# Graph network with cross-attention on one core: turned rows moved into the values' products, weight sums moved to the pair's sums, scores held behind the weighted values, last bias moved into the feed-forward

## The chip, the core and the metric

The kernel runs on 1 core of one Trainium2 chip. Its time is the device time of one execution in microseconds (us); for a set of runs the median is given. Five engines matter: PE (TensorE: matmuls and transposes; PEld is its weight load), DVE (VectorE), ACT (ScalarE), POOL (GpSimd) and SP (SyncE, which here issues nearly all DMAs). Each executes its own instructions in a fixed order and waits on semaphores for the others.

## The reference

N = 1024 rows of D = 512 features pass a layer norm with ReLU, a batch norm and a graph convolution. Then come L = 4 layers, each a cross-attention (16 groups of 64 rows, each with its own M = 256 condition rows, H = 8 heads of DH = 64) and a gated feed-forward block. A second graph convolution and two residuals end it.

```python
for i in range(L):
    a = _attn(_ln(h, ln2_w[i], ln2_b[i]), cond, Wq[i], Wk[i], Wv[i], Wo[i])
    h = h + a
    u = _ln(h, ln3_w[i], ln3_b[i]) @ geglu_w[i] + geglu_b[i]
    val, gate = jnp.split(u, 2, axis=-1)
    f = val * jax.nn.gelu(gate, approximate=False)
    h = h + f @ ffo_w[i] + ffo_b[i]
```

All of it is float32. The bias `ffo_b[i]` is added to `h` once in each layer; nothing reads `h` between the attention's end and the feed-forward's sums except the layer norm of `ln3`, which must not see the bias.

## The kernel before

**Tiling.** The 1024 rows are 8 blocks of 128 rows, `h[0]` to `h[7]`, views of one tile `hall`. A block is also an attention step g (0 to 7): two groups of 64 rows. Most matrix products are done in seven block products instead of eight (Strassen's scheme in Winograd's form), so sums of blocks are made beside them: of weights and of turned rows mostly on POOL, of products on DVE (read from PSUM, where matmuls write), with copies on ACT.

**One attention step** `g` of layer `l` (the loop from line 1198 on): `scores` (L750) multiplies queries by keys of step g (tiles `sc`, L761) and does the softmax: on DVE the row maximum (L768), on ACT the exponential (L773), on DVE the reciprocal (L776) and the scaling of the probabilities (L778, eight instructions of 128x256 from SBUF to SBUF). `kv` (L745) then makes the keys and values of step g+1 with two calls of `seven` (L708): products 0, 5, 6, 4, 1, 3, 2 go to the PSUM banks `pa`, `pb`, `pc`, `pd`, `pa`, `pc`, `pd`, eight matmul records each. In between, DVE makes `u2` (L721) and `u3` (L724) and adds them into the four quarters of the result. Product 3 is accumulated onto `pc`, so it can begin only when `u3` has read that bank. Last, `mix` (L782) turns the probabilities of step g (tiles `tr_pr`, copied out as `pT`, L809 on DVE and L811 on ACT) and weighs the values with them (tiles `po`, L795); its result is `oT`.

**Between the keys and the values** of step g+1 stands `between` (L1207). At every second step `attn_out_pair` (L836) multiplies the two last `oT` with `wo`, again in seven products (`wab`, `wcd`): four sums on POOL ahead of them (L843 to L846, "the pair's sums"), and on POOL again the additions L865, L866, L871 and L874, which finish `h` of two blocks. Then `ln3_norm` (L1175) normalises one finished block (two at step 6) on DVE, from the statistics (L151) to the scaled rows `xn` (L172), and `ln3_bias` (L1184) adds `ffb`, the feed-forward's output bias, to `h` of that block on POOL (L1185). `ln3_turn` (L1187) turns the normalised rows on PE (`tr_ln`, four transposes a block, L184) and writes them to `ln3T` with two ACT and two DVE instructions (L698, L696); `ln3_sums` (L1191) makes the sums `ln3S` of blocks 4 and 5 on POOL (L212 to L215, eight instructions).

**Steps 6 and 7.** At step 6 the first feed-forward weights, `wval` and `wgate`, are loaded and `geglu_weights` (L887) makes their sums `ges` on POOL (L219 to L222, 128x1024 each). In the program that call stands behind `kv`. Step 7 stands behind the loop: its scores, `attn_out` of block 6 (`pw`, L824), the first feed-forward products (`Quad.first`, tiles `ga`) as a filler, `mix`, then the last two blocks.

**The feed-forward** has R = 4 rounds r: four `Quad`s each (tiles `ga` to `gd`), then `ffn_out` twice (tiles `fa` to `fd`), which adds to `h` on DVE and POOL. POOL also makes the weight sums of the rounds to come.

**What sets the order.** The framework places each engine's instructions in one order when the kernel is built, by a simulated execution: of the instructions that the simulation holds ready, the one that is earliest in the program comes first. `tc.issue_after` forbids one engine's instruction to come ahead of another. Tiles of a pool (36 `slots`, 8 PSUM banks) are given out in the order in which the program first writes them, so an instruction that first writes a tile is never placed ahead of an earlier first write of that pool. On the chip the order is fixed, and an instruction waits only for what it really needs, so an engine can run well ahead of the simulation. `ges`, the keys `kT`, the values `v`, `ln3T`, `ln3S` and all weights are tiles of `slots`.

## Time and profile before

| | us |
|---|---|
| median of 3 runs | 2541.16 (2541.14 to 2543.61) |
| the profiled execution, whole | 2541.56 |
| its span, first to last instruction | 2539.7 |
| DVE busy | 1405.7 (55%) |
| POOL busy | 643.4 (25%) |
| ACT busy | 556.2 (22%) |

The profiled execution lies 0.40 us above the median of the runs. A row of a timeline has the start in us from the span's start, the time in us, the engine, the source line, the operation, the tiles (out <- in), the shapes and a count; in brackets stands how long the engine sat idle before it, and for whom. A row of the list of waits has who waited for whom, the total in us, how often, and the longest. Rows that stand together with a count are records: a float32 matmul leaves two. The four layers are alike; in time, layers 2 and 3 repeat layer 1 with a shift of about 588 us each.

### The profile page before, as it was taken

Reading aid. Unit: us, or ns where it says so; the run is one execution under the profiler, and the core shown is the slowest. Engines: PE = TensorE matmul, PEld = TensorE weight load, DVE = VectorE, ACT = ScalarE, POOL = GpSimd, SP = SyncE. Lnnn points to the kernel's source line nnn. Section 1 sums busy time; section 2 is a strip of 40 time slices with the busy share of each in tenths; the row PEclk is TensorE's granted clock in tenths of the full one; section 3 lists DMA queues with packets and bytes.
Section 4 is the critical chain, followed back from the end, with each engine's and each line's share of the span. In section 5 each row is a group of like instructions: output and inputs, shape, how many; then the busy total and the mean of one; then the engine's idle time right before and its main releaser. Section 6 shows DMA issues by size and latency. Waiting matters only on the chain. (4 is left out here: it accounts for less than half of the span.)

```text
span 2539.7 us, 32198 instructions
## 1 busy us (share of the span) xinstructions
PE 2512.0 (99%) x12464; PEld 1770.6 (70%) x12464; DVE 1405.7 (55%) x3030; ACT 556.2 (22%) x1318; POOL 643.4 (25%) x535
## 2 busy tenths in 40 slices
PE   8999999999999999999999999999999999999999
PEld 5778886666578887655587888556676888566565
DVE  9655566544574556544474556644484455654561
ACT  7322222111122222111122222111112222211111
POOL 0322225422210113433320113333320111531410
PEclk9999999999999999999999999999999999999999
DMA  6312231111121111210212111110112121111020
GB/s 178 130 38 84 92 133 63 34 50 37 59 66 68 51 54 51 71 33 17 95 38 79 59 63 51 54 50 17 59 67 75 42 80 60 41 34 62 13 87 34
DMA packets 67136, 156.81 MB, mean 62 GB/s; under 512 B 5576, under 2 KB 5904, under 8 KB 66976
## 3 DMA queue, kind: packets, MB, share of 16 engines
q1 hardware_dynamic: 64880, 149.25, 17.9%
q0 software_dynamic: 1376, 4.30, 0.5%
q8 instruction: 103, 1.69, 0.3%
q10 hardware_dynamic: 720, 1.11, 0.1%
q14 instruction: 57, 0.47, 0.1%
HBM read 133.66 MB, written 20.97 MB: 61 GB/s over the span
## 5 line engine op out<-in xcount | busy, mean ns | idle before, releaser
L301 PE MATMUL ga<-ln3T,wval 128*128 128x512 f32 x512 | 233.9, 593 | 0.0
L923 ACT ACTIVATE g<-g,gcols 128x512 f32<-128x512 f32 x128 | 92.4, 722 | 431.8 <-DVE g L936 367.2
L301 PEld LDWEIGHTS ga<-ln3T,wval 128*128 128x128 f32 x512 | 96.0, 190 | 109.9 <-issue 109.0
L773 ACT ACTIVATE pr<-sc,nmax 128x256 f32<-128x256 f32 x256 | 118.2, 474 | 180.0 <-DVE nmax L768 180.0
L997 POOL TENSOR_TENSOR hall<-fu,hall 128x512 f32<-128x512 f32 x24 | 30.5, 1270 | 468.0 <-DVE fu L996 468.0
L301 PE MATMUL pa_v<-wv,ct 128*128 128x256 f32 x512 | 123.1, 379 | 0.0
L301 PE MATMUL fa<-wff,fT 128*128 128x256 f32 x512 | 121.6, 379 | 0.0
L301 PE MATMUL gc<-ln3S,wgate 128*128 128x512 f32 x256 | 120.4, 592 | 1.1 <-DVE gu L933 1.1
L301 PE MATMUL pd_k<-ct,wks 128*128 128x256 f32 x512 | 121.0, 379 | 0.0
L301 PE MATMUL pd_v<-wvs,ct 128*128 128x256 f32 x512 | 121.0, 379 | 0.0
L301 PE MATMUL pc_k<-ct,wk 128*128 128x256 f32 x512 | 120.9, 379 | 0.0
L301 PE MATMUL pc_v<-wv,ct 128*128 128x256 f32 x512 | 120.9, 379 | 0.0
L301 PE MATMUL gb<-ln3S,ges 128*128 128x512 f32 x256 | 120.6, 593 | 0.0
L301 PE MATMUL gd<-ln3T,ges 128*128 128x512 f32 x256 | 120.5, 593 | 0.0
L301 PE MATMUL gd<-ln3S,ges 128*128 128x512 f32 x256 | 120.3, 592 | 0.0
L301 PE MATMUL gc<-ln3T,wgate 128*128 128x512 f32 x256 | 120.3, 592 | 0.0
L301 PE MATMUL pa_k<-ct,wk 128*128 128x256 f32 x480 | 116.2, 385 | 0.0
L301 PEld LDWEIGHTS fa<-wff,fT 128*128 128x128 f32 x512 | 97.3, 190 | 21.8 <-issue 9.6
L1185 POOL TENSOR_TENSOR hall<-hall,ffb 128x512 f32<-128x512 f32 x28 | 36.1, 1294 | 286.9 <-DVE xn_ln L172 286.9
L301 PEld LDWEIGHTS pd_v<-wvs,ct 128*128 128x128 f32 x512 | 97.3, 190 | 13.2
L301 PEld LDWEIGHTS pc_k<-ct,wk 128*128 128x128 f32 x512 | 97.3, 190 | 13.2
L301 PEld LDWEIGHTS pd_k<-ct,wks 128*128 128x128 f32 x512 | 97.3, 190 | 13.2
(319 smaller groups left out, 4866.7 us busy)
## 6 DMA issues: line engine op xcount, KB each, us to landing
ct<-cond_dram SPq DMA_DIRECT2D x72, 512.0 KB, 4.7
wval<-in_L_gnn_geglu_w_dram SPq DMA_DIRECT2D x32, 512.0 KB, 4.7
wgate<-in_L_gnn_geglu_w_dram SPq DMA_DIRECT2D x32, 512.0 KB, 4.7
wff<-in_L_gnn_ffo_w_dram SPq DMA_DIRECT2D x32, 512.0 KB, 4.5
cond_dram<-ct SPq DMA_DIRECT2D x24, 512.0 KB, 3.6
cond<-in_L_gnn_cond_dram SPq DMA_DIRECT2D x32, 256.0 KB, 4.5
ct<-cond_dram SPq DMA_DIRECT2D x24, 256.0 KB, 4.9
wk<-in_L_gnn_Wk_dram SPq DMA_DIRECT2D x8, 512.0 KB, 5.2
```

Source lines behind the costliest of these rows:

```text
L301: nc.tensor.matmul(at, left[:, k, l0:l1], right[:, k, r0:r1], start=start and n == 0 and k == 0, stop=n == len(cols_of) - 1 and k == 1, sk ...
L773: nc.scalar.activation(pr3[:, a, :], ps3[:, a, :], AF.Exp, bias=nmax[:, a:a + 1], accum_out=tot[:, a:a + 1])
L923: nc.scalar.activation(pre, pre, AF.Gelu, bias=gcols[:, cg:cg + 1])
L997: t.tensor_tensor(h21, halves_of(u2), h21, OP.add)
L1185: t.tensor_tensor(h[nb], h[nb], ffb, OP.add)
```

## The change

Four edits, all of order; each arithmetic operation is done as before, on the same shapes, but the bias of all eight blocks is now added on POOL.

1. `seven` gets a hook `late`, called behind product 1; with the values of step g+1 it turns the rows that `between` has normalised. Before, they were turned behind the values.
2. `attn_out_pair` is split: `pair_sums` has the four POOL sums. At step 6 `geglu_weights` is called between `pair_sums` and the pair's products.
3. The score matmuls of step g (from 1 on) may not be placed ahead of the last matmul of `mix` of step g-1.
4. `ln3_bias` is gone, on POOL behind each normalised block and on DVE for block 7. The eight additions stand on POOL in round 1 of the feed-forward.

```diff
@@ seven
+        late()
         product(3, c, False)
@@ scores
+                        with tc.issue_after(mix.last.ins) if g else nullcontext():
                             nc.tensor.matmul(
@@ mix
-                            nc.tensor.matmul(
+                            mix.last = nc.tensor.matmul(
@@
-    def attn_out_pair(l, g, oTs, right):
+    def pair_sums(l, g, oTs):
...
         t.tensor_tensor(s2, s1, a11, OP.subtract)
         t.tensor_tensor(s4, a12, s2, OP.subtract)
-        left = [a11, a12, s4, a22, s1, s2, a21]
+        return [a11, a12, s4, a22, s1, s2, a21], more[:, M:]
+
+    def attn_out_pair(l, g, left, p1, right):
@@ ln3_norm
-            for nb in blocks:
-                ln3_bias(nb)
-
-        def ln3_bias(nb, t=nc.gpsimd):
-            t.tensor_tensor(h[nb], h[nb], ffb, OP.add)
@@ between
                 if len(oTs) == 2:
-                    attn_out_pair(l, g - 2, oTs, wo7)
+                    blocks = pair_sums(l, g - 2, oTs)
                     oTs.clear()
+                    if g == NG - 2:
+                        left = geglu_weights(l, 0, *raw)
+                    attn_out_pair(l, g - 2, *blocks, wo7)
                 ln3_norm(*ready, behind=last_key)
 
             if g or l:
-                kv_next = kv(l, g + 1, wk, wv, between)
+                kv_next = kv(l, g + 1, wk, wv, between, late=lambda: [ln3_turn(nb) for nb in ready])
             else:
                 kv_next = kT_1, values(0, 1, wv)
-            if g == NG - 2:
-                left = geglu_weights(l, 0, *raw)
             save_conds()
             next_cond(l, g + 2)
             for nb in ready:
-                ln3_turn(nb)
                 if nb >= 4:
                     ln3_sums(nc.gpsimd, nb)
@@ block 7
-        ln3_bias(g, nc.vector)
@@ rounds of the feed-forward, behind the weight sums of the round
+            if r == 1:
+                for nb in range(NB):
+                    nc.gpsimd.tensor_tensor(h[nb], h[nb], ffb, OP.add)
```

More of the change, by code (lines that the diff above doesn't have):

```diff
@@ L284, in next_cond @@
             conds[l, g] = load_cond(l, g) if l else prepare_cond(g)
-    conds = {}
+    conds, left = {}, None
     def blocks_of_w(w):
@@ L706, in weight_sums, with seven @@
         return [blk[0], blk[1], s4, blk[3], s1, s2, blk[2]]
-    def seven(name, product, c11, c12, c21, c22, s1=None, beside=lambda ins: None):
+    def seven(name, product, c11, c12, c21, c22, s1=None, beside=lambda ins: None,
+              late=lambda: None):
         b, c, d = (bank(f"{n}_{name}") for n in ("pb", "pc", "pd"))
@@ L737, in keys, with values, kv @@
         return kT, seven(f"k_{l}_{g}", of_k(wk, conds[l, g]), *blocks_out(kT), s1, *beside)
-    def values(l, g, wv, begun=None):
+    def values(l, g, wv, begun=None, **also):
         v, s1 = begun or (slots_of(2, f"v_{l}_{g}"), None)
         v11, v21, v12, v22 = blocks_out(v)
-        seven(f"v_{l}_{g}", of_v(wv, conds.pop((l, g))), v11, v12, v21, v22, s1)
+        seven(f"v_{l}_{g}", of_v(wv, conds.pop((l, g))), v11, v12, v21, v22, s1, **also)
         return v
-    def kv(l, g, wk, wv, between):
+    def kv(l, g, wk, wv, between, **also):
         kT, last_key = keys(l, g, wk)
         between(last_key)
-        return kT, values(l, g, wv)
+        return kT, values(l, g, wv, **also)
     def scores(l, g, qT, kT):
@@ L760, in scores @@
                     for b in range(2):
-                        nc.tensor.matmul(
-                            banks[2 * c2 + j][b * NPG:(b + 1) * NPG, a * M:(a + 1) * M],
-                            qT[g // 4][c2][pj, a, c0 + b * NPG:c0 + (b + 1) * NPG],
-                            kT[c2][pj, a, b * M:(b + 1) * M], start=True, stop=True)
+                        with tc.issue_after(mix.last.ins) if g else nullcontext():
+                            nc.tensor.matmul(
+                                banks[2 * c2 + j][b * NPG:(b + 1) * NPG, a * M:(a + 1) * M],
+                                qT[g // 4][c2][pj, a, c0 + b * NPG:c0 + (b + 1) * NPG],
+                                kT[c2][pj, a, b * M:(b + 1) * M], start=True, stop=True)
         for u in range(4):
@@ L794, in weigh @@
                             at = (a * MB + m) * P + b * NPG
-                            nc.tensor.matmul(
+                            mix.last = nc.tensor.matmul(
                                 po[j * DH:(j + 1) * DH, n0:n0 + NPG],
@@ L846, in attn_out_pair @@
         t.tensor_tensor(s4, a12, s2, OP.subtract)
-        left = [a11, a12, s4, a22, s1, s2, a21]
+        return [a11, a12, s4, a22, s1, s2, a21], more[:, M:]
+    def attn_out_pair(l, g, left, p1, right):
+        n = f"{l}_{g}"
+        t = nc.gpsimd
         ab, cd = bank(f"wab_{n}"), bank(f"wcd_{n}")
@@ L855, in attn_out_pair @@
         kept = acc_tile(f"ou_{n}")
-        p1, u2, p7 = more[:, M:], kept[:, :M], kept[:, M:]
+        u2, p7 = kept[:, :M], kept[:, M:]
         product(0, a, True)
@@ L1207, in between @@
             def between(last_key):
+                nonlocal left
                 if len(oTs) == 2:
-                    attn_out_pair(l, g - 2, oTs, wo7)
+                    blocks = pair_sums(l, g - 2, oTs)
                     oTs.clear()
+                    if g == NG - 2:
+                        left = geglu_weights(l, 0, *raw)
+                    attn_out_pair(l, g - 2, *blocks, wo7)
                 ln3_norm(*ready, behind=last_key)
             if g or l:
-                kv_next = kv(l, g + 1, wk, wv, between)
+                kv_next = kv(l, g + 1, wk, wv, between, late=lambda: [ln3_turn(nb) for nb in ready])
             else:
                 kv_next = kT_1, values(0, 1, wv)
-            if g == NG - 2:
-                left = geglu_weights(l, 0, *raw)
             save_conds()
```

## The prediction, made before the changed kernel was run

> **What bounds the kernel now.** I read the page's first part, then the list of PE's waits, then PE's timeline in layer 1.

> ```profile
> PE 2512.0 (99%) x12464; PEld 1770.6 (70%) x12464; DVE 1405.7 (55%) x3030; ACT 556.2 (22%) x1318; POOL 643.4 (25%) x535
> PE po L795 <- DVE pT L809: 3.0, 4, 0.8
> ```

> PE is the bound: outside 27.7 of 2539.7 us it has a matmul in work. None of the four edits takes work off PE, so all they can win are waits and badly placed instructions, and all they can lose is a new wait of PE. The second row is the one wait of the layers that comes every time: 0.75 us in each, before `po`. More is hidden inside the busy time, and only the timeline shows it: first three rows of an ordinary step, then step 6, then step 7's `mix`.

> ```profile
> 950.86 2.08 PE L795 MATMUL po<-pT,v 128*64 128x64 f32 x64
> 952.88 1.96 PE L761 MATMUL sc<-kT,qT 64*64 64x256 f32 x32
> 954.77 1.99 PE L301 MATMUL pa_k<-ct,wk 128*128 128x256 f32 x8
> ...
> 963.50 1.89 PE L301 MATMUL pc_k<-ct,wk 128*128 128x256 f32 x8
> ...
> 981.63 1.89 PE L301 MATMUL pc_v<-wv,ct 128*128 128x256 f32 x8
> ...
> 985.09 1.04 PE L184 MATMUL tr_ln<-ident,xn_ln 128*128 128x128 f32 x8
> ...
> 987.80 0.33 PE L795 MATMUL po<-pT,v 128*64 128x64 f32 x2
> 988.06 0.64 PE L761 MATMUL sc<-kT,qT 64*64 64x256 f32 x2
> 988.63 2.08 PE L795 MATMUL po<-pT,v 128*64 128x64 f32 x62
> 990.64 1.95 PE L761 MATMUL sc<-kT,qT 64*64 64x256 f32 x30
> 992.52 3.70 PE L824 MATMUL pw<-wo,oT 128*128 128x512 f32 x8
> ...
> 1003.05 0.33 PE L795 MATMUL po<-pT,v 128*64 128x64 f32 x2
> 1004.12 2.08 PE L795 MATMUL po<-pT,v 128*64 128x64 f32 x62 [0.74 <-DVE pT L809]
> ```

> `po` and `sc` together take 954.77 - 950.86 = 3.91 us in an ordinary step and 992.52 - 987.80 = 4.72 at step 6, where a pair of scores is wedged into `po`. The other engines stand in the way only where PE waits for them: POOL and DVE around step 6.

> ```profile
> 956.13 0.73 POOL L846 TENSOR_TENSOR om<-oT,os 128x256 f32<-128x256 f32 x1
> 970.39 0.73 POOL L865 TENSOR_TENSOR ou<-ou 128x256 f32<-128x256 f32 x1 [13.53 <-DVE ou L864]
> ...
> 980.68 2.66 POOL L1185 TENSOR_TENSOR hall<-hall,ffb 128x512 f32<-128x512 f32 x2 [5.39 <-DVE xn_ln L172]
> 983.30 2.35 POOL L219 TENSOR_TENSOR ges<-wgate,wgate 128x1024 f32<-128x1024 f32 x1
> ...
> 990.48 2.36 POOL L222 TENSOR_TENSOR ges<-wval,ges 128x1024 f32<-128x1024 f32 x1
> ...
> 997.93 0.73 POOL L215 TENSOR_TENSOR ln3S<-ln3T,ln3S 128x256 f32<-128x256 f32 x1
> ```
> ```profile
> 956.52 0.76 DVE L778 TENSOR_SCALAR pr<-pr,inv 128x256 f32<-128x256 f32 x2
> ...
> 959.82 0.68 DVE L721 TENSOR_TENSOR u_k<-pb_k,s_k 128x512 f32<-128x512 f32 x1
> 960.61 0.69 DVE L724 TENSOR_TENSOR u_k<-pc_k,u_k 128x512 f32<-128x512 f32 x1
> ...
> 979.99 1.00 DVE L172 TENSOR_SCALAR xn_ln<-hall,mv_ln,y_ln 128x512 f32<-128x512 f32 x2
> ...
> 994.20 1.58 DVE L778 TENSOR_SCALAR pr<-pr,inv 128x256 f32<-128x256 f32 x2
> ...
> 1015.32 0.69 DVE L1185 TENSOR_TENSOR hall<-hall,ffb 128x512 f32<-128x512 f32 x1
> ```

> POOL idles 13.5 us between the pair's sums and the pair's additions, and makes `ges` and `ln3S` later, up to 998.66, over step 7's softmax. There two scalings take 1.58 us instead of some 0.6, and the softmax's lateness is what `pT` hands on to `po` at 1004.12. POOL's work slows DVE's.

> **Part by part.** *Scores behind `po`, rows turned earlier.* The wedge goes, and `pT` no longer queues behind the four ACT and four DVE writes of `ln3T`: 4.72 - 3.91 = 0.81 us a layer. The transposes cost the same inside the products as behind them (eight in 0.87 us, 985.09 to the next row). At their new place, before product 3 at 981.63, both `xn` are ready (979.99 + 1.00 = 980.99), with 0.64 us to spare; the writes fall where ACT and DVE wait for PE. At step 2 `ln3T`'s first write now stands ahead of SP's four loads of `ct`, so these start a product or two later; they are needed a step (36 us) later: nothing.

> *`po` at step 7.* With `ges` and `ln3S` out of the way the softmax is over some 2 us sooner (1.58 against 0.6 for each of the first two pairs), the wait is 0.74, so all of it goes: two records of an ordinary block take 0.06 us, here 1.07, which gives 1.01 a layer.

> *Bias.* POOL loses 28 instructions and DVE four; 32 come back in round 1.

> ```profile
> L1185 POOL TENSOR_TENSOR hall<-hall,ffb 128x512 f32<-128x512 f32 x28 | 36.1, 1294 | 286.9 <-DVE xn_ln L172 286.9
> 1133.89 1.27 POOL L997 TENSOR_TENSOR hall<-fu,hall 128x512 f32<-128x512 f32 x1 [39.31 <-DVE fu L996]
> ```

> Eight of 1.29 are 10.3 us, and POOL stands idle 39.3 us in that round (second row), so the additions and the weight sums behind them fit; nothing needs that `h` before the next `ffn_out`. SP's load of the `ffb` after next waits longer for its tile, with no user near. Without that cover each would be 10.3 us. DVE's own addition (0.69) lay before block 7's sums; PE has `ga` products there and no wait in the list, so I take 0 of 0 to 0.69 a layer.

> *Weight sums.* This is the edit that decides. By first writes `ges` comes behind the keys' tiles `kT` but ahead of `v`, so in POOL's order it can go right behind the pair's sums, ahead of L865. On the chip POOL will not wait for `kT`: it needs the weights alone.

> ```profile
> 916.60 2.10 SPq L108 DMA_DIRECT2D wgate<-in_L_gnn_geglu_w_dram  x2
> DMA to landing us min/median/max: 4.7/4.9/5.2
> ...
> 366.61 0.98 SPq L108 DMA_DIRECT2D wgate<-in_L_gnn_geglu_w_dram  x2
> DMA to landing us min/median/max: 7.2/7.7/8.1
> ```

> In layer 1 (as in 2 and 3) these landed by 924, so `ges` starts at 956.86, when L846 ends, and runs into step 6's softmax, of which only one DVE scaling is done by then. What a long POOL instruction does to DVE I read where it happened in layer 3, POOL's row and DVE's:

> ```profile
> 2365.00 2.79 POOL L219 TENSOR_TENSOR ges<-wgate,wgate 128x1024 f32<-128x1024 f32 x1
> 2365.51 2.83 DVE L970 TENSOR_TENSOR fs<-fT,fs 128x512 f32<-128x512 f32 x1
> ```

> DVE's 128x512 addition from SBUF to SBUF ended at 2368.34, 0.55 us behind the end of POOL's instruction (2367.79): it stood still until POOL was through. The L778 rows at 994.20 fit: 0.8 us each against POOL instructions of 0.73. So one scaling of 0.3 passes between two POOL instructions of 2.35 (taken as 2.3 of holding). From 957.0, when the first scaling is done: scalings 2, 3, 4 and 5 end at 959.6, 962.2, 964.8 and 967.4; then `ges` is over and three more, with the reciprocals, end at 968.5; `u2` 969.1, `u3` 969.9. PE wants `u3` for product 3 of the keys at 963.50 and waits to 969.95: 6.45 us a layer, in three layers. Behind `u3` in DVE's queue stand the keys' quarters, which PE needs later than that. POOL is done at 967, before the pair's additions could begin. In layer 0 the weights are issued at 366.6 and 367.1 and land at 374 to 375; the softmax there is over (959.9 less 588 is 371.9, and 0.6 later for the longer first pair), and `ges` ends at 384, under 2 us behind the start of the additions, which the next products hide: nothing.

> The bounds of this price: by the L778 row alone each pair costs 1.0 more, 3.9 together; `u3` ended at 961.30, with 2.2 of slack, so PE loses 1.7 a layer. If the additions come before the fourth sum, only three hold DVE: 4.1. I take 6.45, because the POOL instructions are those of the 2365.00 row.

> [...]

> *After the wait.* PE does not come back at full speed:

> ```profile
> 10.06 0.35 PE L397 MATMUL pc<-ident,prow 72*128 72x72 f32 x1 [3.75 <-DMA prow<-in_L_gnn_bn_b_dram]
> ...
> 10.73 3.65 PE L184 MATMUL tr_cond<-ident,cond 128*128 128x128 f32 x16
> ...
> 18.11 1.91 PE L184 MATMUL tr_cond<-ident,cond 128*128 128x128 f32 x16
> ```

> The same 16 transposes took 3.65 us after a start with a pause of 3.75 and 1.91 in the stream: 1.74 lost, though the granted clock shows 1.00 in both stretches. I add 1.74 to each wait of 6.45, with 0 as the other bound.

> [...]

> **The sum**, against the profiled execution's 2541.56: gains 4 x (0.81 + 1.01) = 7.3; losses 3 x (6.45 + 1.74) = 24.6; 2558.9. The runs' median lies 0.4 lower: **2558 us**. Its own range, with the restart left out or a little more, is 2552 to 2562.

> **The rivals.** *(1) Faster:* POOL's order holds `ges` back until the softmax is done. It would begin behind the keys' first copy at about 964.3 instead of 956.9; from any start behind 960 no scaling meets it. It then ends at 973.7, the additions 1.3 us late, `xn` at 982.3, and the transposes wait 0.7: 2541.2 - 7.3 + 4 x 0.7 = 2536.7; if the order of POOL stays as it was, so that this edit does nothing, 2533.9. For it speaks that POOL really left `ges` until 983.30 though the weights lay there since 924; against it, that the tile order explains that and is just what the edit shifts. *(2) Same:* the scalings wait as at 994.20, 1.7 a layer: 2541.2 - 7.3 + 5.1 = 2539. For it speaks the row at 994.20; against it that no L778 met an instruction of 2.35. *(3) Smaller loss:* three sums, or a quick restart: 2541.2 - 7.3 + 3 x 4.1 = 2546 to 2553. *(4) Larger loss:* layer 0 collides too (8.2), or round 1's bias meets DVE: up to 2567.

> **How the numbers follow.** Forecast 0.57, (1) 0.15, (2) 0.07, (3) 0.16, (4) 0.05. Runs of this kernel differ by about 0.1%, so 0.2% (5.1 us) is what can be told from no change. Faster by more: (1) without its upper end, 0.15; within: (2) and the lower end of (3), 0.08; slower 0.77. The range leaves out (1) and part of (4): 2538 to 2564.

> **What would show it.** Right: in layers 1 to 3 POOL's L219 directly behind L846; L778 rows of about 2.6 us each in step 6; PE idle some 6 us before product 3 of the keys of step 7, released by DVE `u_k` L724, with matmuls at double spacing behind it; 64 unbroken `po` records and no wait on `pT`. Wrong: L219 starting behind 960, or L778 rows below 1 us beside it. Then the gains stand alone.

## The result, and the profile after

The changed kernel takes 2556.80 us (median of 6 runs, 2556.08 to 2557.33); the kernel before, run beside it, 2542.77 (6 runs, 2541.14 to 2544.10). The ratio is 1.0055, with a 95% interval of 1.0042 to 1.0068: 14.0 us slower, where 2558 was forecast. The profiled execution spans 2555.1 us, 15.4 more than that of before.

First, from the list of PE's waits in the changed kernel (total us, times, longest), the two that the kernel before did not have:

```profile
PE pc_k L301 <- DVE u_k L725: 12.4, 3, 5.3
...
PE pa_k L301 <- ACT s_k L719: 2.1, 1, 2.1
```

The old wait of `po` for `pT` (3.0 us, 4 times) is no longer in that list. Where the new ones come from is in the timeline of layer 1, step 6 (start and length in us, engine, line, operation, out <- in; in brackets the idle time before it and what ended it):

```profile
954.55 0.73 POOL L849 TENSOR_TENSOR om<-oT,os 128x256 f32<-128x256 f32 x1
954.93 2.85 DVE L781 TENSOR_SCALAR pr<-pr,inv 128x256 f32<-128x256 f32 x2
955.23 2.40 POOL L219 TENSOR_TENSOR ges<-wgate,wgate 128x1024 f32<-128x1024 f32 x1
...
957.71 2.35 POOL L220 TENSOR_TENSOR wgate<-wval,wgate 128x1024 f32<-128x1024 f32 x1
...
958.37 4.19 DVE L781 TENSOR_SCALAR pr<-pr,inv 128x256 f32<-128x256 f32 x2
...
962.49 2.34 POOL L222 TENSOR_TENSOR ges<-wval,ges 128x1024 f32<-128x1024 f32 x1
962.67 2.57 DVE L781 TENSOR_SCALAR pr<-pr,inv 128x256 f32<-128x256 f32 x2
...
965.35 0.62 DVE L781 TENSOR_SCALAR pr<-pr,inv 128x256 f32<-128x256 f32 x2
...
966.67 0.69 DVE L725 TENSOR_TENSOR u_k<-pc_k,u_k 128x512 f32<-128x512 f32 x1
...
967.41 3.78 PE L301 MATMUL pc_k<-ct,wk 128*128 128x256 f32 x8 [5.33 <-DVE u_k L725]
...
970.99 2.58 PE L301 MATMUL pd_k<-ct,wks 128*128 128x256 f32 x8
```

`ges` follows the pair's sums (L849) at once, and its four instructions run without a gap until 964.83. While they last a pair of scalings takes 2.57 to 4.19 us; the first pair behind them takes 0.62. `u_k` ends 2.5 us behind `ges`, at 967.36, and PE has stood for 5.33 us. It comes back at half pace: 3.78 and 2.58 us for two products that take 1.89 each. Two windows of that stretch show the clock (a row has the span, its length, the busy us of PE, PEld, DVE, ACT and POOL with the number of records, the granted clock, the DMA share and GB/s):

```profile
965.54:972.37 6.83, 4.96 (x12) 3.97 (x13) 3.10 (x6) 0.00 (x0) 0.00 (x0) 0.50 0.05 6
...
974.00:980.00 6.00, 6.00 (x29) 5.05 (x29) 1.99 (x5) 0.74 (x2) 2.17 (x3) 1.00 0.34 103
```

The clock was halved while PE still stood, at 965.54, and was full again at 972.37. Elsewhere in the timelines of PE, POOL and DVE: first the gains, then the bias, then the two places that differ from layer 1:

```profile
994.25 2.08 PE L798 MATMUL po<-pT,v 128*64 128x64 f32 x64
996.26 1.96 PE L764 MATMUL sc<-kT,qT 64*64 64x256 f32 x32
998.15 3.70 PE L827 MATMUL pw<-wo,oT 128*128 128x512 f32 x8
...
1008.68 2.09 PE L798 MATMUL po<-pT,v 128*64 128x64 f32 x64
...
1071.21 4.95 POOL L1277 TENSOR_TENSOR hall<-hall,ffb 128x512 f32<-128x512 f32 x4
...
1083.29 4.94 POOL L1277 TENSOR_TENSOR hall<-hall,ffb 128x512 f32<-128x512 f32 x4
...
1138.30 1.27 POOL L1005 TENSOR_TENSOR hall<-fu,hall 128x512 f32<-128x512 f32 x1 [34.64 <-DVE fu L1004]
...
1548.81 4.95 DVE L781 TENSOR_SCALAR pr<-pr,inv 128x256 f32<-128x256 f32 x2
1548.83 2.35 POOL L219 TENSOR_TENSOR ges<-wgate,wgate 128x1024 f32<-128x1024 f32 x1
...
1556.06 3.66 PE L301 MATMUL pa_k<-ct,wk 128*128 128x256 f32 x8 [2.11 <-ACT s_k L719]
1561.43 1.99 PE L301 MATMUL pc_k<-ct,wk 128*128 128x256 f32 x8 [1.71 <-DVE u_k L725]
...
2394.67 1.93 PE L301 MATMUL fd<-wffs,fs 128*128 128x256 f32 x6 [1.90 <-DVE fs L977]
2396.39 3.25 PE L301 MATMUL fb<-wffs,fs 128*128 128x256 f32 x8
```

`po` and `sc` of step 6 take 998.15 - 994.25 = 3.90 us, unbroken, and step 7's `po` runs as one block without a wait. The eight bias additions of round 1 end at 1088.2, nobody waits for them, and POOL is still idle for 34.64 us behind that round's sums. In layer 2 `ges` begins together with the first scaling, and the delay is split between two waits. In layer 3's round 2 the wait of 1.90 us is the one that the kernel before had too, but there the products behind it kept their pace, and here they lose 1.7 us at half the clock.

How far PE stands behind the kernel before, at the same matmul of both timelines (us):

| place | before | after | shift |
|---|---|---|---|
| layer 0, `po` of step 6 | 399.75 | 400.49 | +0.74 |
| layer 0, `fa` of round 0 | 472.58 | 471.25 | -1.33 |
| layer 1, `po` of step 5 | 950.86 | 949.28 | -1.58 |
| layer 1, first product of the pair (`wab`) | 966.96 | 973.40 | +6.44 |
| layer 1, feed-forward | 1055.43 | 1059.83 | +4.40 |
| layer 2, `pb_k` of step 6 | 1544.20 | 1548.61 | +4.41 |
| layer 2, `wab` | 1554.56 | 1564.99 | +10.43 |
| layer 2, feed-forward | 1645.18 | 1653.57 | +8.39 |
| layer 3, `pb_v` of step 5 | 2113.76 | 2121.82 | +8.06 |
| layer 3, `wab` | 2142.49 | 2158.21 | +15.72 |
| layer 3, round 1 | 2263.72 | 2277.39 | +13.67 |
| layer 3, round 2 | 2394.49 | 2409.84 | +15.35 |
| last matmul | 2535.30 | 2550.69 | +15.39 |

So layers 1 to 3 lose 8.02, 6.02 and 7.66 at the keys, 21.7 together; each of the four layers gains 2.04 to 2.07 behind that, 8.2 together: 13.5. The rest of the 15.4 is 1.7 in layer 3's round 2, 0.74 that stands there before any edited step matters, and two small gains of 0.3. The gain of a layer has three parts, the same in all four: 0.82 at step 6 (4.72 to 3.90), 1.06 at `po` of step 7 (3.08 to 2.02 until the next product), and 0.17 at `gb`, the first product that reads block 7's sums `ln3S`. From the start of the `ga` before it to the start of the `gc` behind it PE takes 5.34 us before (1015.69 to 1021.03) and 5.16 after (1020.26 to 1025.42). Where DVE adds the bias, it does so ahead of those sums.

### The profile page after: what moved, and what is told of

Read it like the earlier page. It is cut to its first block, busy times and chain, and to the rows that moved or that the text cites. A ratio compares the mean times of both kernels' runs of the same rounds, so it can differ in the third digit from the quotient of the medians.

```text
span 2555.1 us, 32224 instructions
## 1 busy us (share of the span) xinstructions
PE 2516.4 (98%) x12464; PEld 1773.5 (69%) x12464; DVE 1428.2 (56%) x3026; ACT 558.0 (22%) x1318; POOL 646.6 (25%) x539
## 5 line engine op out<-in xcount | busy, mean ns | idle before, releaser
L301 PE MATMUL ga<-ln3T,wval 128*128 128x512 f32 x512 | 233.9, 593 | 0.0
L301 PEld LDWEIGHTS ga<-ln3T,wval 128*128 128x128 f32 x512 | 96.0, 190 | 109.9 <-issue 109.1
L846 POOL TENSOR_TENSOR os<-oT 128x256 f32<-128x256 f32 x12 | 8.7, 728 | 566.8 <-DVE oT L821 566.8
L301 PE MATMUL pc_k<-ct,wk 128*128 128x256 f32 x512 | 124.8, 388 | 12.4 <-DVE u_k L725 12.4
L301 PE MATMUL pa_v<-wv,ct 128*128 128x256 f32 x512 | 123.1, 379 | 0.0
L301 PE MATMUL pd_k<-ct,wks 128*128 128x256 f32 x512 | 121.9, 381 | 0.0
L301 PE MATMUL fa<-wff,fT 128*128 128x256 f32 x512 | 121.6, 379 | 0.0
L301 PE MATMUL gc<-ln3S,wgate 128*128 128x512 f32 x256 | 120.4, 592 | 1.1 <-DVE gu L941 1.1
L301 PE MATMUL pc_v<-wv,ct 128*128 128x256 f32 x512 | 121.0, 379 | 0.0
L301 PE MATMUL pd_v<-wvs,ct 128*128 128x256 f32 x512 | 121.0, 379 | 0.0
L301 PE MATMUL gd<-ln3T,ges 128*128 128x512 f32 x256 | 120.6, 593 | 0.0
L301 PE MATMUL gb<-ln3S,ges 128*128 128x512 f32 x256 | 120.3, 592 | 0.0
L301 PE MATMUL gc<-ln3T,wgate 128*128 128x512 f32 x256 | 120.3, 592 | 0.0
L301 PE MATMUL gd<-ln3S,ges 128*128 128x512 f32 x256 | 120.3, 592 | 0.0
L301 PE MATMUL pa_k<-ct,wk 128*128 128x256 f32 x480 | 118.0, 389 | 2.1 <-ACT s_k L719 2.1
L301 PEld LDWEIGHTS pc_k<-ct,wk 128*128 128x128 f32 x512 | 99.2, 194 | 27.6 <-DVE u_k L725 13.8
L301 PEld LDWEIGHTS fa<-wff,fT 128*128 128x128 f32 x512 | 97.3, 190 | 21.8 <-issue 9.6
L301 PEld LDWEIGHTS pd_k<-ct,wks 128*128 128x128 f32 x512 | 98.3, 192 | 13.7
L781 DVE TENSOR_SCALAR pr<-pr,inv 128x256 f32<-128x256 f32 x256 | 104.9, 452 | 2.9
```

The lines of the kernel that those rows point to most:

```text
L301: nc.tensor.matmul(at, left[:, k, l0:l1], right[:, k, r0:r1], start=start and n == 0 and k == 0, stop=n == len(cols_of) - 1 and k == 1, sk ...
L781: nc.vector.tensor_scalar(pr3[:, a, :], pr3[:, a, :], inv[:, a:a + 1], None, OP.mult)
L846: t.tensor_tensor(s1, a21, a22, OP.add)
```

## The experiments

My theory: POOL's long additions of `ges` hold DVE's softmax scalings, and this alone makes the loss. Rivals: the transposes inside the values or the scores behind `po` cost it; or POOL's traffic in SBUF slows every engine. Four kernels first, on one chip, with the kernel before at 2542.31 (17 runs).

**Hold `ges` back** (`sums_gated`). `scores.last` is the last scaling of a step; `waiting_for` makes POOL's instructions of the block wait for it.

```diff
                     if g == NG - 2:
-                        left = geglu_weights(l, 0, *raw)
+                        with waiting_for(scores.last, mybir.EngineType.Pool):
+                            left = geglu_weights(l, 0, *raw)
```

> The changed kernel, with the same order on every engine, but the four instructions of ges in attention carry a wait for the last DVE scaling of step 6 (L781). My theory: ges runs from about 960 to 969.5 in layer 1's clock of before, where DVE has no work from SBUF to SBUF that PE waits for soon; POOL's first pair addition comes at most 1 us late; no wait before product 3 of the keys: 2556.8 - 21.7 - 1.7 = 2533, range 2532 to 2538, faster than before by 0.2 to 0.4%. Rival (the place of ges in POOL's order is harmless and the loss has another cause): 2553 to 2558.

Measured: 2534.18 (6 runs, 2532.50 to 2536.00), ratio 0.9970, interval 0.9957 to 0.9982. Its timeline, step 6 of layer 1:

```profile
956.75 0.62 DVE L781 TENSOR_SCALAR pr<-pr,inv 128x256 f32<-128x256 f32 x2
...
957.45 2.36 POOL L219 TENSOR_TENSOR ges<-wgate,wgate 128x1024 f32<-128x1024 f32 x1 [3.12 <-DVE pr L781]
...
958.07 0.69 DVE L725 TENSOR_TENSOR u_k<-pc_k,u_k 128x512 f32<-128x512 f32 x1
...
960.97 1.89 PE L301 MATMUL pc_k<-ct,wk 128*128 128x256 f32 x8
...
964.62 2.35 POOL L222 TENSOR_TENSOR ges<-wval,ges 128x1024 f32<-128x1024 f32 x1
...
967.85 0.73 POOL L873 TENSOR_TENSOR ou<-ou 128x256 f32<-128x256 f32 x1 [0.87 <-DVE ou L872]
```

POOL gives up 3.12 us, the scalings end at 957.37, `u_k` runs at full pace beside `ges` (0.69 us; it reads one operand from PSUM), and PE has no wait. The order on PE, DVE and ACT is that of the changed kernel, and only POOL's start differs: the loss of 22 us hangs on it. POOL is even idle again before the pair's additions.

**Half of it** (`two_sums`). The first two instructions of the `ges` of attention go at once, the last two carry the wait.

```diff
-        sums_of_a(nc.gpsimd, *wval, *wgate, *s)
+        if r:
+            sums_of_a(nc.gpsimd, *wval, *wgate, *s)
+        else:
+            t, (a11, a12), (a21, a22) = nc.gpsimd, wval, wgate
+            t.tensor_tensor(s[0], a21, a22, OP.add)
+            t.tensor_tensor(a21, a11, a21, OP.subtract)
+            with waiting_for(scores.last, mybir.EngineType.Pool):
+                t.tensor_tensor(s[1], s[0], a11, OP.subtract)
+                t.tensor_tensor(s[2], a12, s[1], OP.subtract)
```

> The changed kernel; the first two instructions of ges run at once as there, the last two carry the wait for the last scaling of step 6. A dose test. My theory (each instruction of ges holds DVE for its 2.35 us): in layers 1 and 3 of the changed kernel u_k (L725) ended 2.5 us behind the end of the fourth instruction; here 2.5 to 3.3 behind the end of the second, so PE waits 0.5 to 1.3 instead of 5.33, without the slow stretch behind it: 2534 to 2540. Rival (the four instructions together aren't what counts; one is enough for the whole loss): 2550 to 2557.

Measured: 2539.76 (10 runs, 2537.78 to 2540.68), ratio 0.9989, interval 0.9979 to 0.9998. The timeline of layer 1:

```profile
957.20 2.35 POOL L902 TENSOR_TENSOR wgate<-wval,wgate 128x1024 f32<-128x1024 f32 x1
...
962.11 0.69 DVE L725 TENSOR_TENSOR u_k<-pc_k,u_k 128x512 f32<-128x512 f32 x1
...
962.86 1.99 PE L301 MATMUL pc_k<-ct,wk 128*128 128x256 f32 x8 [1.28 <-DVE u_k L725]
```

The second instruction ends at 959.55 and `u_k` at 962.80, 3.25 us behind it; PE waits 1.28 in layers 1 and 3, and no half clock follows. Layer 2 keeps its wait of 2.11 for `s_k`, so two instructions are enough for that one. The dose is what the theory asks for.

**The scalings on ACT** (`scaled_on_act`). `ges` stays where the changed kernel has it.

```diff
-                nc.vector.tensor_scalar(pr3[:, a, :], pr3[:, a, :], inv[:, a:a + 1], None, OP.mult)
+                if g == NG - 2:
+                    nc.scalar.activation(pr3[:, a, :], pr3[:, a, :], AF.Copy, scale=inv[:, a:a + 1])
+                else:
+                    nc.vector.tensor_scalar(pr3[:, a, :], pr3[:, a, :], inv[:, a:a + 1], None, OP.mult)
```

> The changed kernel; at step 6 the eight scalings of the softmax are made by ACT, at every other step by DVE as before. ges stays where the changed kernel has it. My theory (POOL and DVE exclude each other, ACT is not concerned): the ACT scalings take about 0.47 us each beside POOL's instructions of 2.35, the softmax ends at about 960.5 in layer 1's clock of before, s_k behind it on ACT some 0.6 later, and PE waits at most 1 to 1.5 a layer: 2534 to 2543. Rival (POOL's traffic in SBUF slows whoever reads and writes there): the ACT scalings too take 1 us and more, 2548 to 2560.

Measured: 2533.35 (6 runs, 2532.28 to 2534.77), ratio 0.9965, interval 0.9953 to 0.9978. Timeline, layer 1:

```profile
955.13 2.36 POOL L219 TENSOR_TENSOR ges<-wgate,wgate 128x1024 f32<-128x1024 f32 x1
...
956.16 0.92 ACT L782 ACTIVATE pr<-pr,inv 128x256 f32<-128x256 f32 x2
...
960.53 0.69 DVE L725 TENSOR_TENSOR u_k<-pc_k,u_k 128x512 f32<-128x512 f32 x1
...
961.81 1.89 PE L301 MATMUL pc_k<-ct,wk 128*128 128x256 f32 x8
```

`ges` starts as early as in the changed kernel, and ACT's scalings take 0.46 each beside it, as long as its exponentials elsewhere (0.47), where DVE's took 2.57 to 4.19 a pair in the changed kernel. PE has no wait at the keys at all, where I had allowed up to 1.5 us, and the time is just below my range. Here POOL hinders DVE and not ACT: the rival of general traffic falls.

**`ges` behind the values again** (`sums_back`), the other three edits kept.

```diff
-                    if g == NG - 2:
-                        left = geglu_weights(l, 0, *raw)
                     attn_out_pair(l, g - 2, *blocks, wo7)
...
+            if g == NG - 2:
+                left = geglu_weights(l, 0, *raw)
             save_conds()
```

> The changed kernel with one part undone: the gate weights' sums (ges) stand behind the values again; the turn inside the values, the scores behind po and the moved bias stay. POOL's order differs from the changed kernel only there. My theory (ges on POOL holds DVE's scalings of step 6, which delays u_k): no wait of PE before product 3 of the keys, L781 rows of step 6 at 0.6 each pair, so the 8.0, 6.0 and 7.7 us that layers 1 to 3 lose in the changed kernel are gone: 2556.8 - 21.7 - 1.7 (the slow stretch in layer 3's round 2) = 2533 at best. But ges now begins right behind the pair's last addition (about 976 in layer 1's clock of before) and meets the two row scalings xn (L172) that end at 981: each can be held for up to 2.35, PE then waits up to 3 us a layer before the transposes inside the values: 2533 to 2546. Rival (the loss comes from the transposes inside the products or from the scores behind po): still 2553 to 2558.

Measured: 2565.05 (4 runs, 2563.70 to 2566.86), ratio 1.0091, interval 1.0074 to 1.0108: slower than the changed kernel, and outside both expectations. The wait at the keys is gone, as I expected, but the new one is dearer. Timeline of layer 1:

```profile
981.50 2.35 POOL L219 TENSOR_TENSOR ges<-wgate,wgate 128x1024 f32<-128x1024 f32 x1
981.57 1.29 DVE L151 BATCH_NORM_STATS2 st_ln<-hall 128x6 f32<-128x512 f32 x2 [0.83 <-POOL hall L882]
...
984.11 2.19 DVE L139 SCALAR_TENSOR_TENSOR a_ln<-y_ln,v_ln 128x2 f32<-128x2 f32 x1
...
986.23 0.68 DVE L722 TENSOR_TENSOR u_v<-pb_v,s_v 128x512 f32<-128x512 f32 x1
...
988.84 2.19 DVE L139 SCALAR_TENSOR_TENSOR a_ln<-y_ln,v_ln 128x2 f32<-128x2 f32 x1
991.06 0.16 DVE L141 TENSOR_TENSOR b_ln<-a_ln,y_ln 128x2 f32<-128x2 f32 x1
...
993.21 1.94 PE L184 MATMUL tr_ln<-ident,xn_ln 128*128 128x128 f32 x8 [5.16 <-DVE xn_ln L172]
```

I had counted two held scalings of rows, and overlooked the chain of tiny operations before them: the root for two row blocks works on tiles of two numbers a partition, 0.16 us each, and some of these are held about as long as a POOL instruction takes (2.19 beside 2.35). PE waits 5.16 us before the transposes in each of the four layers (20.7 in its list), again with half the clock behind. In the kernel before, the bias additions kept `ges` off until 983.30, when the root was done. So with the bias gone and the rows turned inside the values, the old place of `ges` is worse than the new one. How much of it the earlier turn costs, no run tells.

Four more kernels followed, three of them single edits, with the kernel before at 2542.97 (24 runs).

**The weight sums alone** (`sums_alone`: the kernel before with `geglu_weights` between the pair's sums and its products):

```diff
...
-                    attn_out_pair(l, g - 2, oTs, wo7)
+                    blocks = pair_sums(l, g - 2, oTs)
                     oTs.clear()
+                    if g == NG - 2:
+                        left = geglu_weights(l, 0, *raw)
+                    attn_out_pair(l, g - 2, *blocks, wo7)
...
-            if g == NG - 2:
-                left = geglu_weights(l, 0, *raw)
```

> The kernel before with the second edit alone: ges between the pair's sums and the pair's products. My theory: layers 1 to 3 lose at the keys what they lose in the changed kernel (8.0, 6.0 and 7.7 us, a few tenths more or less), and since ges no longer runs over step 7's softmax, that step's wait of 0.74 before po goes (1.05 a layer with it); the scores wedged into po stay: 2542.3 + 21.7 - 4.2 = 2559.8, range 2556 to 2563. Rival (the loss needs the other edits too, since they move the DVE's work of step 6): 2538 to 2548.

Measured: 2559.63 (4 runs, 2558.64 to 2560.22), ratio 1.0068, interval 1.0052 to 1.0083. In its list of waits:

```profile
PE pc_k L301 <- DVE u_k L724: 16.0, 3, 5.3
```

All three layers wait 5.33 here, and `po` no longer waits for `pT`: the second edit makes the whole loss, and also the gain at step 7.

**The scores alone** (`scores_alone`): `tc.issue_after(mix.last.ins)` around the scores' matmuls, in the kernel before.

```diff
-                        nc.tensor.matmul(
...
+                        with tc.issue_after(mix.last.ins) if g else nullcontext():
+                            nc.tensor.matmul(
...
-                            nc.tensor.matmul(
+                            mix.last = nc.tensor.matmul(
```

> The kernel before with the third edit alone: a group's scores issued behind the last product of the values before them. My theory: po runs unbroken in step 6 (3.91 instead of 4.72 us), and nothing else moves: 0.81 a layer, 2542.3 - 3.2 = 2539.1, range 2537 to 2541.5; the wait of po for pT at step 7 stays at about 0.7. Rival (the wedged pair filled a hole, and unbroken po waits for pT at step 6): no gain, 2541 to 2544.

Measured: 2539.35 (11 runs, 2538.83 to 2541.50), ratio 0.9988, interval 0.9979 to 0.9997.

**The turn alone** (`turn_alone`): the hook `late` in the values, in the kernel before.

```diff
...
+        late()
         product(3, c, False)
...
-                kv_next = kv(l, g + 1, wk, wv, between)
+                kv_next = kv(l, g + 1, wk, wv, between, late=lambda: [ln3_turn(nb) for nb in ready])
...
-                ln3_turn(nb)
```

> The kernel before with the first edit alone: the normalised rows are turned inside the values, the bias additions and ges stand where they were. My theory: step 6's pT no longer queues behind the writes of ln3T, so the scheduler need not wedge scores into po (up to 0.81 a layer less); ges and the sums of ln3S still run over step 7's softmax, so that wait stays, perhaps shorter, since ln3S can begin some 5 us sooner: 2536 to 2543, most likely 2539. Rival (the transposes in the values come before xn is ready): a new wait at tr_ln, 2543 to 2548.

Measured: 2539.57 (11 runs, 2539.05 to 2541.32), ratio 0.9991, interval 0.9982 to 1.0000. Step 6 of layer 1 in PE's timeline, first with the scores alone, then with the turn alone:

```profile
986.64 2.50 PE L796 MATMUL po<-pT,v 128*64 128x64 f32 x64
989.07 1.96 PE L762 MATMUL sc<-kT,qT 64*64 64x256 f32 x32
990.95 3.70 PE L825 MATMUL pw<-wo,oT 128*128 128x512 f32 x8
```
```profile
987.30 2.08 PE L797 MATMUL po<-pT,v 128*64 128x64 f32 x64
989.32 1.96 PE L763 MATMUL sc<-kT,qT 64*64 64x256 f32 x32
991.21 3.70 PE L826 MATMUL pw<-wo,oT 128*128 128x512 f32 x8
```

Either edit removes the wedged scores. With the scores alone `po` is stretched to 2.50, since `pT` still queues behind the writes of `ln3T`: 4.31 for the two instead of 4.72. With the turn alone it is 3.91, the whole 0.81. But its wait before `po` of step 7 grew from 0.74 to 0.92, where I had thought it might shrink; with the scores alone it is 0.66. The runs give 3.6 and 3.4 us, too close to tell the two apart; the trace says that for step 6 the turn suffices.

**The bias back in attention** (`gated_bias_back`), in the kernel with `ges` held back.

```diff
+            for nb in blocks:
+                ln3_bias(nb)
...
-            if r == 1:
-                for nb in range(NB):
-                    nc.gpsimd.tensor_tensor(h[nb], h[nb], ffb, OP.add)
```

> The version with the held-back ges (sums_gated), with the fourth edit undone: the bias additions stand in attention again (28 on POOL, four on DVE). My theory: they ran in POOL's idle time and cost 0 to 0.7 a layer, so 2534.2 to 2537. Rival (a gain of the changed kernel comes from the bias: POOL's two additions of 1.27 each behind the pair's additions meet the DVE scalings of the row blocks or of step 7's softmax, as ges did): a wait before po or tr_ln of 1 us and more a layer, 2538 to 2545.

Measured: 2534.80 (7 runs, 2534.16 to 2536.28), ratio 0.9970, interval 0.9959 to 0.9981; with the bias in round 1 it was 2534.18. The runs show no effect of the fourth edit. The traces, with PE's matmuls in the same order, show a small gain: 5.32 us from `ga` to `gc` at block 7's sums with the bias on DVE (1012.09 to 1017.41) and 5.15 without (1011.28 to 1016.43), 0.17 in each of the four layers.

**The waits of layer 3** (`base_later`). The kernels so far keep two waits in layer 3's round 2, 1.06 before `gc` and 1.90 before `fd`. `ffn_out.last` is the last addition of an `ffn_out`; the edit is made on top of the held-back `ges`.

```diff
-    for nb in range(NB):
-        nc.gpsimd.tensor_tensor(base[nb], base[nb], bias_out, OP.add)
+    with waiting_for(ffn_out.last, mybir.EngineType.Pool):
+        for nb in range(NB):
+            nc.gpsimd.tensor_tensor(base[nb], base[nb], bias_out, OP.add)
```

> sums_gated, and in the last layer the eight POOL additions base + bias_out (L1314 of the changed kernel) carry a wait for the last addition of the last ffn_out; the order of PE and DVE is that of sums_gated. In all kernels so far they stand ahead of round 2's ges in POOL's order, which therefore begins at 2356 in sums_gated, and its additions hold DVE up: PE waits 1.06 and 1.89 us (gc and fd). My theory: ges then begins some 30 us sooner, as in the other layers, both waits go, and with them the stretch at half the granted clock that follows the longer wait in some executions (1.7 us): 2534.2 - 3.0 - some 0.8 = 2530.4, range 2529 to 2532, and the executions of this kernel lie closer together (within 2 us, where sums_gated's lay within 3.5). Rival (the two waits come from DVE's own order, not from POOL): 2533 to 2536 and the same waits. The additions at the end can cost at most what they hold of the last stage: it has no DVE work with two operands in SBUF.

Measured: 2529.84 (5 runs, 2528.89 to 2530.27) against 2542.83 (9 runs), ratio 0.9947, interval 0.9934 to 0.9961: the fastest of all. In POOL's timeline:

```profile
2318.18 2.35 POOL L219 TENSOR_TENSOR ges<-wgate,wgate 128x1024 f32<-128x1024 f32 x1
...
2462.99 9.85 POOL L1316 TENSOR_TENSOR base<-base,bias_out 128x512 f32<-128x512 f32 x8 [32.74 <-DVE hall L1014]
```

`ges` begins 38 us sooner than in the kernel with `ges` held back (2355.98), right behind round 1's sums, where six of DVE's first eight operations in the changed kernel read from PSUM (2343.03 to 2352.37); both waits are gone from the list. The runs lie within 1.4 us, where the kernel without this edit spread over 3.5.

## Why the prediction held, step by step

- *POOL's order and the collision.* As forecast: L219 directly behind the pair's sums, scalings of 2.6 us and more, `u_k` late, PE idle before product 3, in layers 1 to 3 and not in layer 0. `sums_gated` and `sums_alone` show that the place of `ges` makes all of the loss, `two_sums` that it goes with the number of instructions, `scaled_on_act` that DVE is the engine concerned (0.46 us a scaling on ACT).
- *The wait of 6.45.* 5.33 in layers 1 and 3. The forecast let a POOL instruction and a held scaling take turns at 2.6 us. In fact the scaling slips in between two POOL instructions without delaying them: `ges` goes through at 2.4 an instruction (9.60 for the four, 9.54 in the kernel before, at 983.30, where no scaling stood beside it). So `u_k` ended 12.1 us behind the start of `ges`, where 13.0 was forecast.
- *Three equal layers.* This step failed in layer 2. There L219 began with the first scaling (1548.83 and 1548.81), so both scalings of the first pair were held (4.95 us for the two), the next maxima came late, ACT's exponentials behind them, and `s_k` behind these. PE stopped earlier, for 2.11, and again for 1.71: 6.0 in place of 7.7 to 8.0. With the second edit alone layer 2 waited 5.33 like the others, so it is a matter of some tenths of a microsecond in when `ges` begins.
- *The restart, 1.74 a wait.* (3.78 - 1.89) + (2.58 - 1.89) = 2.6 in layer 1, 2.2 in layer 3, 1.8 in layer 2, with the granted clock at 0.50. That PE comes back slow was right, and the size is that of one stretch: the trace's clock entries show 3.41 us of half clock in layer 2 (1556.05 to 1559.46) and 6.83 in layers 1 and 3 (965.54 to 972.37, 2149.97 to 2156.80), of which PE worked 4.96 and 4.20. The forecast took the size from the start of the kernel, where the view prints a clock of 1.00; there the trace has no clock entry at all before 14.92 us. The 16 transposes ahead of it started 0.21 us apart, the later ones 0.11, and in `sums_alone` and `base_later` the spacing changes just where the entries begin (12.84 and 13.19). So that row too was most likely at half the clock; that its length fitted one stretch was luck.
- *The gains, 1.82 a layer.* 2.05. The wait at step 7 gave 1.06, near the 1.01, and the 0.81 of step 6 is there once, though two edits each bring it. The other 0.17 is the bias.
- *Bias.* Free on POOL, as forecast: its additions of 4.95 and 4.94 us went into idle time, of which 34.64 us are left behind them where the kernel before had 39.31. On DVE it was not free before: of the 0 to 0.69 a layer for which the forecast took 0, 0.17 came back (`gated_bias_back`).
- *The sum.* 24.6 - 7.3 = 17.3 was forecast, 21.7 - 8.2 = 13.5 came. Both errors made the forecast too slow, the loss by 2.9 and the gain by 0.9; the runs' medians differ by 14.0. That 2558 is only 1.2 off owes something to the kernel before, whose median beside the changed kernel was 2542.77 and not the 2541.16 that the sum was set against.

The rival that the order of POOL would hold `ges` back is what `sums_gated` made true: it gives 2534.18, inside the 2534 to 2537 of that rival.

## What to carry to other kernels

As this case shows, filling an idle stretch of POOL is not free while DVE has work from SBUF to SBUF in it (2.57 to 4.19 us a pair of scalings beside `ges`, 0.62 behind it): look at which operands DVE reads (`u_k`, with one in PSUM, kept its 0.69), not at POOL's busy share. Where a long POOL job has slack, give it a wait for the last DVE operation that matters (22 us here for one line), or move that operation to ACT (0.46 us a scaling, 2533.35 for the kernel). A list of instructions ordered by first use will start such a job at the earliest moment, which is a moment chosen by nobody.

## What was not expected of the hardware

The size of a DVE operation did not matter here for being held: one of two numbers a partition took 2.19 us beside a POOL addition, 0.16 alone. Of the operations in the same rows, those that read PSUM (`u_v`, 0.68) and the statistics (L151, two in 1.29) were not held: their means in the changed kernel are 0.69, and 0.69 for one. POOL was the slower one too: in the kernel before, its L219 at 2365.00 took 2.79 behind a DVE addition begun at 2363.95 (L969, 1.64), where the other fifteen took 2.35 on average.

Half the clock followed a wait of 5.2 to 5.3 us of PE each time (nine of nine, in the changed kernel, `sums_back` and `sums_alone`), and the waits of 2.11 before `pa_k` both times (the changed kernel, `two_sums`). After the wait of 1.90 before `fd` it came in two of ten profiles, the changed kernel's and this one, of `gated_bias_back`:

```profile
2373.33 2.78 PE L301 MATMUL fd<-wffs,fs 128*128 128x256 f32 x6 [1.90 <-DVE fs L977]
2375.90 2.40 PE L301 MATMUL fb<-wffs,fs 128*128 128x256 f32 x8
```

Without it the six records took 1.56 and the next eight 1.89. Two waits near the start, which every kernel has, did it at times too: that before `hw_in` (1.58 to 1.90) in three of eleven profiles, that before `pa_kT` (1.82 to 2.29) in one, where it was 1.98.
